# The seam between two stacks: pools ordered by lifetime, the last blocks' sum and norm as small steps of the following stack, and projections drawn ahead

## The chip, the cores and the metric

The kernel runs on one core of a Trainium2 chip, in float32 throughout. A core has a matrix engine (TensorE, PE in the profile), a vector engine (VectorE, DVE), a scalar engine (ScalarE, ACT), a general engine (GpSimd, POOL) and a queue processor (SyncE, SP) that issues most transfers. Each engine works through its own list of instructions in order; semaphores make one wait for another. The metric is the device time of one execution in microseconds (us); less is better.

## The reference

A block of two stacks over x of shape (B, S, D) = (2, 2048, 256), with a modulation that is drawn from a condition vector:

```python
mod = (silu(c) @ wmod).reshape(B, 6, 1, D)       # sa, ca, ga, sb, cb, gb
h = layernorm(x) * (1 + ca) + sa
x = x + ga * favor_stack(h)      # 3 layers: causal linear attention, 16 heads; MLP 256-1024-256
h = layernorm(x) * (1 + cb) + sb
x = x + gb * local_stack(h)      # 2 layers: attention in windows of 128, 8 heads; gated MLP
```

In the first stack each layer is post-norm: `h = LN(out + attention)`, `out = LN(h + mlp(h))`. In the second, queries, keys and values come from a token-shifted h (half the features from the token before), q and k are normalised and rotated, a softmax runs over the own and the former window, and the gated MLP follows on another token shift and norm. The third and fourth lines of the code meet at the seam of this study: the sum `x + ga * ...`, its layer norm, and the first projections of the local stack.

## The kernel before

**Two stages, two scopes.** The first `with ExitStack() as c1` holds the favor stack, the second (`c2`) the local stack. The first works in blocks of TA = 256 tokens: `favor_block(b, n)` for b in 2 batches and n in 8 blocks, three calls of `favor_layer` in each. The blocks are generators, and `planned` (L91) interleaves up to four of them by due times; the order on PE is the order in which they are drawn, while DVE, ACT and POOL of this stage are ordered by a scheduler. The local stack works in tiles of 128 tokens: `attn_tile` (L815) returns a dictionary of small operations, each with a due time in tiles in `WHEN` (L124), and all operations of all tiles, with those of the MLP (`mlp`, from L1182), are sorted by due time and drawn in that order on PE, DVE, ACT and POOL. "k" at 0.398 and "v" at 1.887, for instance, mean that a tile's k projection is drawn 0.4 tiles, and its v projection 1.9 tiles, after its q projection.

**The end of a favor block.** After layer 2, `favor_layer` returns the normed deviation `dn` (the function `normed`, L409: bn_stats and bn_aggr on DVE, Ln and Exp of the variance on ACT, subtract and multiply on DVE, L421). `favor_block` then makes `x1 = scaled(...)` (L437: three POOL operations, L442, L444 and L445, with rows that are broadcast over the partitions in `brow`), stores x1 to `xmid` in DRAM (L753), norms it again (`normed(x1)`), transposes it on PE (`turned`, L426), applies the second modulation on ACT into `hm` (L435), and stores hm to `hmid` in DRAM (L758).

**The start of the local stack.** `entry` (L789 to L795) holds the streams of 2 x 4 blocks of 512 tokens, each a tile of two rows of 512 features-by-token and a column between them for the token shift; each is loaded from `hmid` by two transfers (L794), and its shift column is copied on POOL from the block before (L783). Then come a mask (L799) and `w2` of the MLP (L199). A tile's start is: `q`, `k`, `v` (L860, two program instructions each, four in the profile), `cosq`/`cosk` (DVE, L872), `cq`/`ck`/`cv` (copies on ACT, L883 and L888), `sq` (ACT), `rot` (POOL, L902), `red` (DVE, L912), `ln` (ACT), `add` (POOL, L924), `nrm` (DVE, L929), `tp` (transposes on PE, L939), `qT` and `kT`, the scores `s0`/`s1` (L956), their maxima (L972), `ng` (L988), the exponentials (L996), `nm` (POOL, L1011), the transposes `p0`/`p1` (L1023), `av` (L1049), `oT` (DVE, L1060) and `po` (L1068).

**Memory.** The SBUF pools of the second scope take the addresses that the first scope has left, in the order in which they are opened: first the streams (`strm`, 16 tiles of 4.1 KB a partition), then weights, then work tiles. PSUM is one pool of eight banks in the second scope (`bank`, L775), taken in turn. The tag `wb1` of the shared pool holds favor layer 1's weights and later the MLP's `w1` (`load_mlp`, L184), which is loaded by `next_weights` (L721) while the favor stack still runs its last layers.

Of the kernel before, what the change touches and what calls it, by code (L numbers as in the profile page):

```python
# [14 lines left out]
P = 128  # L15
# [24 lines left out]
def block_kernel(ctx: ExitStack, tc: tile.TileContext, t: dict, out: bass.AP):  # L40
# [50 lines left out]
    def planned(jobs, at_once):  # L91
# [41 lines left out]
    }  # L133
    FEED = 0.32

    def parked(name, shape):
# [59 lines left out]

    def load_w2(pool, l):
        w2 = pool.tile([P, NFH, D], F32, tag="w2", name="w2")
        nc.sync.dma_start(  # L199
            w2[:, : NFH - 1, :], t["w2"][l, :AW, :].rearrange("(k p) n -> p k n", p=P)  # L200
        )

        for m in range(KT):
            nc.sync.dma_start(
                w2[G_AT * m : G_AT * m + GW, NFH - 1, m * P : (m + 1) * P],
                t["w2"][l, AW:, m * P : (m + 1) * P],
            )
        return w2

    attn_w, mlp_w = {}, {}  # L210


    with ExitStack() as c1:
# [9 lines left out]
        def load_x(b, n):  # L223
            xin = work.tile([P, NCA, D], F32, tag="xin", name="xin", bufs=3)
            nc.sync.dma_start(
                xin, x_in[b, n * TA : (n + 1) * TA, :].rearrange("(c p) d -> p c d", p=P)
            )
            return xin
# [177 lines left out]
            load_weights(2, "Wq", "Wk", "Wv", "Wo", "W1", "W2")  # L406
            yield 0.2, 0.0

        def normed(src):  # L409

            mv = sp.tile([P, NCA, 2], F32, tag="mv", name="mv")
            for c in range(NCA):
                bs = sp.tile([P, 6], F32, tag="bs", name="bs")
                nc.vector.bn_stats(bs, src[:, c, :])
                nc.vector.bn_aggr(mv[:, c, :], bs)
            rs = sp.tile([P, NCA], F32, tag="rs", name="rs")
            nc.scalar.activation(rs, mv[:, :, 1], AF.Ln, bias=eps_t)
            nc.scalar.activation(rs, rs, AF.Exp, scale=-0.5)
            dn = work.tile([P, NCA, D], F32, tag="dn", name="dn", bufs=3)
            for c in range(NCA):  # L420
                nc.vector.tensor_scalar(  # L421
                    dn[:, c, :], src[:, c, :], mv[:, c, 0:1], rs[:, c : c + 1], ALU.subtract, ALU.mult
                )
            return dn
# [37 lines left out]
        def favor_layer(b, n, l, h, hres):  # L462
# [245 lines left out]
            s = work.tile([P, NCA, D], F32, tag="s", name="s2")  # L708
            for c in range(NCA):
                nc.vector.tensor_tensor(s[:, c, :], acc[:, c, :], hres[:, c, :], ALU.add)  # L710
            dn = normed(s)
            yield 0.86, 3.9
            if l == LA - 1:
                return dn, None
# [17 lines left out]
        def favor_block(b, n):  # L732
            if (b, n) == (0, 0):
                dn, h = h_first
            else:
                dn = normed(early.pop((b, n)) if (b, n) in early else load_x(b, n))
                yield 0.0, 4.0
                h = hp.tile([P, KT, TA], F32, tag="h", name="h0")
                turned(dn, h, lambda k: mod[:, 1, k, b : b + 1], lambda k: mod[:, 0, k, b : b + 1])
            hres = partial(scaled, dn, R_G0 + b, R_B0 + b)  # L740
            if n > 0:
                hres = hres()
            yield 0.5, 0.9, "attention", (b, n - 1, 0) if n else None
# [21 lines left out]


    with ExitStack() as c2:

        strm = c2.enter_context(tc.tile_pool(name="strm", bufs=2 * B * NB))
        wp = c2.enter_context(tc.tile_pool(name="wF", bufs=1))  # L770
        work = c2.enter_context(tc.tile_pool(name="workF", bufs=8))
        ap_ = c2.enter_context(tc.tile_pool(name="attF", bufs=2))
        psum = c2.enter_context(tc.tile_pool(name="psF", bufs=1, space=PSUM))

        def bank(name):  # L775
            return psum.tile([P, TB], F32, tag="ps", name=name, bufs=8)

        def new_stream(b, n, before):
            s = strm.tile([P, 2 * TB + 2], F32, tag="s", name=f"s_{b}_{n}")
# [10 lines left out]
        for b in range(B):  # L790
            for n in range(NB):
                s = new_stream(b, n, entry.get((b, n - 1)))
                for kt in range(KT):
                    nc.sync.dma_start(rows(s)[kt], hmid[b, n][:, kt, :])  # L794
                entry[b, n] = s  # L795

        win_r = wp.tile([P, 2 * P], F32, name="win_r")
        for i in range(2):
            nc.gpsimd.tensor_copy(win_r[:, i * P : (i + 1) * P], win[:, (1 - i) * P : (2 - i) * P])  # L799
        w2s = {0: load_w2(wp, 0)}  # L800
        streams = [entry, {}]
        mids = [{}, {}]
        vals = {}
# [11 lines left out]
        def attn_tile(l, b, n, c):  # L815
# [68 lines left out]

            @op("cv")
            def _():
                vt = new("v", [P, INNER], bufs=5)
                nc.scalar.copy(vt, got["pq", 2])  # L888
                vals[l, b, ti] = vt

# [17 lines left out]

            @op("red")
            def _():  # L910
                ss = new("ss", [P, 2 * NH])
# [340 lines left out]
                return done and (b, n, *done)  # L1252

        steps, start = [], 0.0
        NT, NM = B * nt, B * NB * NFH
        for l in range(LF):
            for i in range(NT):
                ops = attn_tile(l, i // nt, i % nt // NCH, i % NCH)  # L1260
                steps += [(start + i + WHEN[k], l, i, f) for k, f in ops.items()]
# [135 lines left out]
```

## Time and profile before

| | us |
|---|---|
| median of the runs (2979.21 to 2981.54) | 2979.69 |
| the profiled execution | 2982.33 |
| its span, first to last instruction | 2980.5 |
| PE busy | 2909.9 (98%) |
| DVE, ACT, POOL busy | 1681.2, 1339.6, 1067.1 |
| mean granted TensorE clock | 0.99 |

The page's busy time is a mean over the span; DVE at 56% overall is at some 77% in local attention. The slices of the page cut the span into 40 parts of 74.5 us: the favor stack fills slices 0 to 20, the local stack's attention of layer 0 the slices 22 to 26, its MLP 27 to 30, and the second layer the rest.

Around the seam the chain of work that ended last runs through these steps (start, length, what):

```
1564.28 0.76 DVE s L710 x2
1566.51 0.75 DVE dn L421 x2
1567.33 1.26 POOL res L444
1568.67 1.27 POOL res L445
1571.53 0.42 DVE dn L421
1572.09 1.15 PE ntp L431 x4
1574.31 2.43 DMA h<-hm
1576.88 2.68 DMA s<-h
1579.70 6.10 PE pqkv L860 x8
```

In the timeline a row is one group of equal instructions in a row: start, the time it took, engine, line, operation, tiles, partitions x columns, how many. A float32 matmul of the program stands there as two, a transpose as one.

### The profile page before, as it was taken

The numbers are of one execution on the slowest core, as the hardware profiler recorded it, in microseconds if no ns is written. First come the engines' busy times: TensorE is split into PE (matmuls) and PEld (weight loads), VectorE is DVE, ScalarE is ACT, GpSimd is POOL, SyncE is SP. The second block draws the span as 40 slices with busy tenths as digits, with TensorE's granted clock in tenths as the row PEclk, the third lists the DMA queues.
The fourth block names the chain that finished last, engine by engine and source line by source line (L and its number), as shares of the span: only waits on it lengthen the run. The fifth ranks groups of instructions, "written<-read, shape, count | busy, mean of one in ns | idle before, by whom it ended". The sixth has DMA issues, their size and how long they took to land.

```text
span 2980.5 us, 49140 instructions
## 1 busy us (share of the span) xinstructions
PE 2909.9 (98%) x19323; PEld 2128.4 (71%) x19323; DVE 1681.2 (56%) x4186; ACT 1339.6 (45%) x3263; POOL 1067.1 (36%) x942
## 2 busy tenths in 40 slices
PE   8999999999999999999996999999999999999999
PEld 6888887888888888888784777775444777776444
DVE  5555556555665556655534777774224777775222
ACT  3343344343443334343334667665114666766211
POOL 4222233222422223322324666663002666663000
PEclk9999999999999999999998999999999999999999
DMA  6000010000100001001012000001000000000011
GB/s 217 1 1 1 8 36 15 1 1 1 43 16 1 1 1 36 22 1 43 23 34 77 1 1 1 1 1 58 0 0 10 20 1 1 2 1 8 28 43 36
DMA packets 38327, 59.48 MB, mean 20 GB/s; under 512 B 3854, under 2 KB 29008, under 8 KB 37456
## 3 DMA queue, kind: packets, MB, share of 16 engines
q1 hardware_dynamic: 36288, 52.37, 5.3%
q8 instruction: 153, 2.51, 0.3%
q0 software_dynamic: 992, 2.92, 0.3%
q10 hardware_dynamic: 816, 1.05, 0.1%
q14 instruction: 78, 0.64, 0.1%
HBM read 43.72 MB, written 12.60 MB: 19 GB/s over the span
## 4 chain that ended last, share of the span: by engine, by line
PE 89%; DVE 4%; ACT 3%; POOL 2%; issue 1%; DMA 1%; ACTq 0%; POOLq 0%; DVEq 0%; SPq 0%
PE acc L698 11%; PE pf L687 10%; PE pqkv L860 10%; PE pg L1205 5%; PE pq L475 5%; PE acc L1243 5%; PE pa L1205 4%; PE av L1049 4%; PE sim L956 3%; PE ptp L1023 3%; PE po L1068 3%; PE nd L635 3%; PE sc L563 3%; PE pu L516 3%; PE po L665 3%; PE pv L491 3%
## 5 line engine op out<-in xcount | busy, mean ns | idle before, releaser
L698 PE MATMUL acc<-wb,fr 128*128 128x256 f32 x1536 | 398.5, 382 | 7.0 <-ACT fr L695 5.1
L687 PE MATMUL pf<-h,wa 128*128 128x256 f32 x1536 | 402.4, 385 | 0.6 <-DVE att L569 0.3
L695 ACT ACTIVATE fr<-pf,vec 128x256 f32<-128x256 f32 x384 | 180.6, 471 | 427.1 <-PE pf L687 426.3
L860 PE MATMUL pqkv<-wqkv,s 128*128 128x512 f32 x768 | 357.3, 601 | 6.5 <-DMA s<-h 6.5
L569 DVE TENSOR_TENSOR att<-sc,cst 128x512 f32<-128x512 f32 x384 | 238.3, 683 | 158.0 <-PE sc L563 158.0
L698 PEld LDWEIGHTS acc<-wb,fr 128*128 128x128 f32 x1536 | 288.8, 190 | 54.0 <-ACT fr L695 8.6
L444 POOL TENSOR_TENSOR res<-dn,brow 128x512 f32<-128x512 f32 x112 | 145.1, 1295 | 486.0 <-DVE dn L421 479.4
L687 PEld LDWEIGHTS pf<-h,wa 128*128 128x128 f32 x1536 | 277.3, 191 | 55.5 <-issue 19.8
L1011 POOL TENSOR_TENSOR pm<-pm,sum 128x1024 f32<-128x1024 f32 (+1 forms) x128 | 235.5, 1840 | 179.6 <-DVE sum L1006 179.6
L996 ACT ACTIVATE pm<-pm,mx 128x256 f32<-128x256 f32 (+1 forms) x512 | 249.4, 488 | 59.2 <-DVE mx L988 59.0
L860 PEld LDWEIGHTS pqkv<-wqkv,s 128*128 128x128 f32 x768 | 138.0, 193 | 133.9 <-issue 132.0
L902 POOL TENSOR_TENSOR rot<-raw,rsn_wo 128x512 f32<-128x512 f32 x128 | 160.3, 1273 | 180.8 <-ACT raw L883 180.5
L1214 DVE SCALAR_TENSOR_TENSOR ge<-pa,vec,ge 128x512 f32<-128x512 f32 x80 | 60.1, 751 | 282.9 <-PE pa L1205 231.6
L1213 ACT ACTIVATE ge<-pg,vec 128x512 f32<-128x512 f32 x96 | 65.8, 685 | 316.5 <-PE pg L1205 316.5
L487 ACT ACTIVATE xs<-xs 64x512 f32<-64x512 f32 x192 | 120.6, 628 | 152.3 <-DVE xs L486 143.0
L1205 PE MATMUL pg<-s,w 128*128 128x512 f32 (+1 forms) x384 | 182.2, 597 | 0.0
L475 PE MATMUL pq<-h,wa 128*128 128x256 f32 x768 | 176.2, 383 | 0.7 <-ACT h L435 0.7
L486 DVE TENSOR_TENSOR xs<-pq,vec 64x512 f32<-64x512 f32 x192 | 132.1, 688 | 75.3 <-PE pq L475 71.5
L1243 PE MATMUL acc<-ge,w 128*128 128x512 f32 (+1 forms) x384 | 168.8, 600 | 0.0
L475 PEld LDWEIGHTS pq<-h,wa 128*128 128x128 f32 x768 | 146.7, 192 | 22.6 <-issue 1.4
L924 POOL TENSOR_TENSOR qk<-qk,rot 128x1024 f32<-128x1024 f32 x64 | 151.3, 2363 | 0.5
L1205 PE MATMUL pa<-s,w 128*128 128x512 f32 x320 | 150.4, 592 | 0.0
(163 smaller groups left out, 5339.7 us busy)
## 6 DMA issues: line engine op xcount, KB each, us to landing
xin<-in_x_dram SPq DMA_DIRECT2D x32, 256.0 KB, 2.8
x<-res SPq DMA_DIRECT2D x16, 256.0 KB, 2.1
h<-hm SPq DMA_DIRECT2D x16, 256.0 KB, 2.4
s<-h SPq DMA_DIRECT2D x16, 256.0 KB, 4.8
xl<-x SPq DMA_DIRECT2D x8, 512.0 KB, 4.3
out_dram<-res SPq DMA_DIRECT2D x8, 512.0 KB, 3.2
w<-in_w_dram SPq DMA_DIRECT2D x6, 640.0 KB, 3.9
wa<-in_W_dram SPq DMA_DIRECT2D x3, 1024.0 KB, 8.3
```

Of the source, the lines that this page charges most:

```text
L475: nc.tensor.matmul(pq[:, g, :], W[wn, l][:, kt, g * P : (g + 1) * P], h[:, kt, :], start=(kt == 0), stop=(kt == KT - 1),)
L569: nc.vector.tensor_tensor(am, scs[i].rearrange("p g q c -> p (g q) c"), caus.unsqueeze(1).to_broadcast([P, 2 * KT, P]), ALU.mult,)
L687: nc.tensor.matmul(pf, W["W1", l][:, kt, f * P : (f + 1) * P], h1[:, kt, :], start=(kt == 0), stop=(kt == KT - 1),)
L695: nc.scalar.activation(fr[f], pf, AF.Relu, bias=v("bf1", f))
L698: nc.tensor.matmul(acc[:, c, :], fr[f - 1][:, c * P : (c + 1) * P], W["W2", l][:, f - 1, :], start=(f == 1 and c == 0), stop=(f == NF), sk ...
L860: nc.tensor.matmul(pq, s[:, kt * TB + c * P : kt * TB + (c + 1) * P], wqkv[:, kt, i * INNER : (i + 1) * INNER], start=(kt == 0), stop=(kt ...
L902: nc.gpsimd.tensor_tensor(rot[:, :, :, lo : lo + 32], got["raw"][:, :, :, hi : hi + 32], rsn[:, ti, :, lo : lo + 32].unsqueeze(2).to_broad ...
L924: nc.gpsimd.tensor_tensor(got["qk"], got["qk"], got["rot"], ALU.add)
L996: nc.scalar.activation(pm[:, hd, :], pm[:, hd, :], AF.Exp, bias=of("mx", hg)[:, hd : hd + 1], accum_out=of("sum", hg)[:, hd : hd + 1],)
L1011: nc.gpsimd.tensor_tensor(pm, pm, of("sum", hg).unsqueeze(2).to_broadcast([P, 4, kw]), ALU.mult)
L1205: nc.tensor.matmul(pt[:m, :], w1[:, kt, off : off + m], hb[:, kt * TB : (kt + 1) * TB], start=(kt == 0), stop=(kt == KT - 1),)
L1243: nc.tensor.matmul(acc[m], w2[rs_, f, m * P : (m + 1) * P], g[rs_, :], start=(f == 0), stop=(f == NFH - 1),)
```

## The change

- **Pools.** In the second scope the work tiles (`work`), a new pool for v and the sums of squares (`vp_`) and a pool for the first four streams (`strm0`) are opened first, then the other twelve streams (`strm1`), then the rest. In the first scope, the small tiles of `normed` move from the pool `sp` to `work`.
- **The last blocks.** For the last block of each batch (n = 7), `favor_block` ends after layer 2. Its `dn` is written into a tile `last`, which takes the place of favor layer 1's weights (tag `wb1`); x of these blocks and the four rows of gains and biases are loaded there ahead. The sum, its store to `xmid`, the statistics, the norm, the transposes and the modulation become eleven steps for each batch, in the list of the local stack's layer 0 at tiles 3 + 3b to 6.6 + 3b. The tokens go straight into the stream in SBUF, not through `hmid`.
- **Streams.** Only block (0, 0) is loaded ahead of the list; the seven others are drawn at tile 1.1. The shift column comes from `hmid` by a transfer of one column instead of a copy on POOL. The mask is drawn at tile 2.
- **First projections.** `FIRST` shifts the due times of some projections of tiles 0 to 3, with the operations that take their result.
- **MLP weights.** `w1` and `w2` are loaded at tile 12 of each layer; before, layer 0's came at the end of the favor stack and the start of the local one, layer 1's at tile 4.

```diff
+    FIRST = [
+        {"v": -1.1},
+        {"q": -0.58, "k": -0.45, "v": -1.59},
+        {"q": -0.97, "k": -0.3, "v": -1.56},
+        {"q": -0.96, "k": -0.18},
+    ]
+    TAKES = {"q": ("cosq", "cq"), "k": ("ck", "cosk"), "v": ("cv",)}
...
-        def normed(src):
+        def normed(src, dn=None):
...
-            dn = work.tile([P, NCA, D], F32, tag="dn", name="dn", bufs=3)
+            if dn is None:
+                dn = work.tile([P, NCA, D], F32, tag="dn", name="dn", bufs=3)
...
-            dn = normed(s)
+            ends = l == LA - 1 and n == S // TA - 1
+            dn = normed(s, last[0][:, b] if ends else None)
...
-                mlp_w[0] = load_mlp(0)
+                room = shared.tile([P, ROOM], F32, tag="wb1", name="last")
...
+                for b in range(B):
+                    nc.sync.dma_start(
+                        last[1][:, b], x_in[b, S - TA :, :].rearrange("(c p) d -> p c d", p=P)
+                    )
+                nc.gpsimd.dma_start(
+                    last[2].rearrange("p a d -> p (a d)"),
+                    rows_out[R_GE * KT :].rearrange("a c -> (a c)").partition_broadcast(P),
+                )
...
             if n == S // TA - 1:
                 next_weights()
+                return
...
-        strm = c2.enter_context(tc.tile_pool(name="strm", bufs=2 * B * NB))
+        work = c2.enter_context(tc.tile_pool(name="workF", bufs=8))
+        vp_ = c2.enter_context(tc.tile_pool(name="valF", bufs=5))
+        strms = [
+            c2.enter_context(tc.tile_pool(name=f"strm{i}", bufs=k)) for i, k in enumerate((NB, NS - NB))
+        ]
...
+        def load_stream(b, n):
+            s = entry[b, n] = stream_tile(f"s_{b}_{n}")
+            own = slice(0, TB if n < NB - 1 else TB - TA)
+            if n == 0:
+                nc.gpsimd.memset(s[:, TB : TB + 1], 0.0)
+            else:
+                nc.sync.dma_start(s[:, TB : TB + 1], hmid[b, n - 1][:, 1, TB - 1 :])
+            for kt in range(KT):
+                nc.sync.dma_start(rows(s)[kt][:, own], hmid[b, n][:, kt, own])
+
+        load_stream(0, 0)
...
+        def last_sum(b, i):
+            dn, x, rows_ = last[0][:, b], last[1][:, b], last[2]
+            if i == 0:
+                nc.gpsimd.tensor_tensor(
+                    x, x, rows_[:, B + b].unsqueeze(1).to_broadcast([P, NCA, D]), ALU.add
+                )
+            elif i == 1:
+                nc.gpsimd.tensor_tensor(
+                    dn, dn, rows_[:, b].unsqueeze(1).to_broadcast([P, NCA, D]), ALU.mult
+                )
+            else:
+                nc.gpsimd.tensor_tensor(x, x, dn, ALU.add)
+                nc.sync.dma_start(xmid[b, NB - 1][:, NCH - NCA :, :], x)
...
+            nc.vector.bn_stats(bs, last[1][:, b, c, :])
+            nc.vector.bn_aggr(last_mv[b][:, :2, c], bs)
...
+        def last_norm(b, c):
+            m = last_mv[b][:, :, c : c + 1]
+            nc.vector.tensor_scalar(
+                last[0][:, b, c, :], last[1][:, b, c, :], m[:, 0], m[:, 2], ALU.subtract, ALU.mult
+            )
...
+        def last_tokens(b, kt):
+            nc.scalar.activation(
+                rows(entry[b, NB - 1])[kt][:, TB - TA :],
+                last_tp[b][:, kt, :],
+                AF.Identity,
+                bias=mod[:, 3, kt, b : b + 1],
+                scale=mod[:, 4, kt, b : b + 1],
+            )
...
-                if l > 0 and i == NCH:
+                when = dict(WHEN)
+                for k, shift in FIRST[i].items() if l == 0 and i < len(FIRST) else ():
+                    for k2 in (k, *TAKES[k]):
+                        when[k2] += shift
+                steps += [(start + i + when[k], l, i, f) for k, f in ops.items()]
+                if i == 3 * NCH:
                     steps.append((start + i, l, i, partial(load_mlp_late, l)))
+            if l == 0:
+                for b in range(B):
+                    steps += [
+                        (start + 3 + 3 * b + w, l, b, partial(f, b, *a))
+                        for w, f, *a in (
+                            (0.0, last_sum, 0), (0.46, last_sum, 1), (0.96, last_sum, 2),
+                            (1.5, last_stats, 0), (2.05, last_stats, 1), (2.3, last_dev),
+                            (2.5, last_norm, 0), (3.05, last_norm, 1), (3.41, last_turn),
+                            (3.42, last_tokens, 0), (3.6, last_tokens, 1),
+                        )
+                    ]
+                steps.append((start + 2.0, l, 0, turn_mask))
+                blocks = [(b, n) for b in range(B) for n in range(NB)][1:]
+                steps += [(start + 1.1, l, i, partial(load_stream, *blk)) for i, blk in enumerate(blocks)]
```

More of the change, by code (lines that the diff above doesn't have):

```diff
@@ L208, in load_w2 @@
         return w2
-    attn_w, mlp_w = {}, {}
+    attn_w, mlp_w, last = {}, {}, []
     with ExitStack() as c1:
@@ L407, in rest_of_setup @@
             yield 0.2, 0.0
-        def normed(src):
-            mv = sp.tile([P, NCA, 2], F32, tag="mv", name="mv")
+        def normed(src, dn=None):
+            mv = work.tile([P, NCA, 2], F32, tag="mv", name="mv")
             for c in range(NCA):
-                bs = sp.tile([P, 6], F32, tag="bs", name="bs")
+                bs = work.tile([P, 6], F32, tag="bs", name="bs")
                 nc.vector.bn_stats(bs, src[:, c, :])
                 nc.vector.bn_aggr(mv[:, c, :], bs)
-            rs = sp.tile([P, NCA], F32, tag="rs", name="rs")
+            rs = work.tile([P, NCA], F32, tag="rs", name="rs")
             nc.scalar.activation(rs, mv[:, :, 1], AF.Ln, bias=eps_t)
             nc.scalar.activation(rs, rs, AF.Exp, scale=-0.5)
-            dn = work.tile([P, NCA, D], F32, tag="dn", name="dn", bufs=3)
+            if dn is None:
+                dn = work.tile([P, NCA, D], F32, tag="dn", name="dn", bufs=3)
             for c in range(NCA):
@@ L725, in next_weights @@
                 attn_w[0] = load_attn(0)
-                mlp_w[0] = load_mlp(0)
+                room = shared.tile([P, ROOM], F32, tag="wb1", name="last")
+                for i in range(2):
+                    last.append(
+                        room[:, i * B * NCA * D : (i + 1) * B * NCA * D].rearrange(
+                            "p (b c d) -> p b c d", b=B, c=NCA
+                        )
+                    )
+                last.append(
+                    room[:, 2 * B * NCA * D : (2 * B * NCA + 2 * B) * D].rearrange(
+                        "p (a d) -> p a d", d=D
+                    )
[8 more added lines that the diff above has]
+                )
             elif len(late) == 2 * B:
@@ L767, in block_kernel, with stream_tile @@
     with ExitStack() as c2:
-        strm = c2.enter_context(tc.tile_pool(name="strm", bufs=2 * B * NB))
+        NS = 2 * B * NB
+        work = c2.enter_context(tc.tile_pool(name="workF", bufs=8))
[3 more added lines that the diff above has]
+        ]
         wp = c2.enter_context(tc.tile_pool(name="wF", bufs=1))
-        work = c2.enter_context(tc.tile_pool(name="workF", bufs=8))
         ap_ = c2.enter_context(tc.tile_pool(name="attF", bufs=2))
         psum = c2.enter_context(tc.tile_pool(name="psF", bufs=1, space=PSUM))
+        turns = [0]
+        def stream_tile(name):
+            k = int(turns[0] % NS >= NB)
+            turns[0] += 1
+            return strms[k].tile([P, 2 * TB + 2], F32, tag="s", name=name)
         def bank(name):
@@ L778, in new_stream @@
         def new_stream(b, n, before):
-            s = strm.tile([P, 2 * TB + 2], F32, tag="s", name=f"s_{b}_{n}")
+            s = stream_tile(f"s_{b}_{n}")
             if before is None:
@@ L789, in block_kernel, with turn_mask @@
         entry = {}
[L790 to L795, printed above, removed]
+        def load_stream(b, n):
[8 more added lines that the diff above has]
+        load_stream(0, 0)
         win_r = wp.tile([P, 2 * P], F32, name="win_r")
-        for i in range(2):
-            nc.gpsimd.tensor_copy(win_r[:, i * P : (i + 1) * P], win[:, (1 - i) * P : (2 - i) * P])
-        w2s = {0: load_w2(wp, 0)}
+        def turn_mask():
+            for i in range(2):
+                nc.gpsimd.tensor_copy(win_r[:, i * P : (i + 1) * P], win[:, (1 - i) * P : (2 - i) * P])
+        w2s = {}
         streams = [entry, {}]
@@ L886, in _ @@
             def _():
-                vt = new("v", [P, INNER], bufs=5)
+                vt = vp_.tile([P, INNER], F32, tag="v", name="v")
                 nc.scalar.copy(vt, got["pq", 2])
@@ L910, in _ @@
             def _():
-                ss = new("ss", [P, 2 * NH])
+                ss = got["ss"] = vp_.tile([P, 2 * NH], F32, tag="ss", name="ss", bufs=2)
                 nc.vector.tensor_reduce(ss, got["sq"], AX.X, ALU.add)
@@ L1252, in second, with last_stats, last_dev, last_turn @@
                 return done and (b, n, *done)
+        def last_sum(b, i):
[7 more added lines that the diff above has]
+                    dn, dn, rows_[:, b].unsqueeze(1).to_broadcast([P, NCA, D]), ALU.mult
+                )
+            else:
+                nc.gpsimd.tensor_tensor(x, x, dn, ALU.add)
+                nc.sync.dma_start(xmid[b, NB - 1][:, NCH - NCA :, :], x)
+        last_mv = {}
+        def last_stats(b, c):
+            if c == 0:
+                last_mv[b] = vp_.tile([P, 3, NCA], F32, tag="lastmv", name="lastmv", bufs=2)
+            bs = vp_.tile([P, 6], F32, tag="lastbs", name="lastbs", bufs=2)
+            nc.vector.bn_stats(bs, last[1][:, b, c, :])
+            nc.vector.bn_aggr(last_mv[b][:, :2, c], bs)
+        def last_dev(b):
+            rs = last_mv[b][:, 2, :]
+            nc.scalar.activation(rs, last_mv[b][:, 1, :], AF.Ln, bias=eps_t)
+            nc.scalar.activation(rs, rs, AF.Exp, scale=-0.5)
+        def last_norm(b, c):
+            m = last_mv[b][:, :, c : c + 1]
+            nc.vector.tensor_scalar(
+                last[0][:, b, c, :], last[1][:, b, c, :], m[:, 0], m[:, 2], ALU.subtract, ALU.mult
+            )
+        last_tp = {}
+        def last_turn(b):
+            tp = last_tp[b] = bank("ntp").rearrange("p (k c) -> p k c", k=KT)
+            for kt in range(KT):
+                for c in range(NCA):
+                    nc.tensor.transpose(
+                        tp[:, kt, c * P : (c + 1) * P],
+                        last[0][:, b, c, kt * P : (kt + 1) * P],
+                        ident,
+                    )
+        def last_tokens(b, kt):
[5 more added lines that the diff above has]
+                scale=mod[:, 4, kt, b : b + 1],
+            )
         steps, start = [], 0.0
@@ L1260, in block_kernel @@
                 ops = attn_tile(l, i // nt, i % nt // NCH, i % NCH)
-                steps += [(start + i + WHEN[k], l, i, f) for k, f in ops.items()]
-                if l > 0 and i == NCH:
-                    steps.append((start + i, l, i, partial(load_mlp_late, l)))
+                when = dict(WHEN)
[4 more added lines that the diff above has]
+                if i == 3 * NCH:
+                    steps.append((start + i, l, i, partial(load_mlp_late, l)))
+            if l == 0:
[7 more added lines that the diff above has]
+                            (3.42, last_tokens, 0), (3.6, last_tokens, 1),
+                        )
+                    ]
+                steps.append((start + 2.0, l, 0, turn_mask))
+                blocks = [(b, n) for b in range(B) for n in range(NB)][1:]
+                steps += [(start + 1.1, l, i, partial(load_stream, *blk)) for i, blk in enumerate(blocks)]
             at = start + NT
```

## The prediction

> **What bounds the kernel now.** I read the page's slices first, then busy time in stretches around the one slice that stands out, then TensorE's timeline there.
>
> ```profile
> PE   8999999999999999999996999999999999999999
> PEclk9999999999999999999998999999999999999999
> ```
>
> TensorE is full but for slice 21 (1564 to 1639 us), the seam of the two stacks. In stretches (busy us of each engine, granted clock, DMA share, GB/s):
>
> ```profile
> 1555.50:1564.20 8.70, 7.96 (x38) 6.39 (x36) 1.12 (x5) 3.32 (x9) 0.00 (x0) 1.00 0.08 31
> 1564.20:1631.40 67.20, 42.04 (x210) 24.76 (x210) 31.18 (x90) 24.06 (x69) 28.66 (x31) 0.80 0.24 85
> 1631.40:1645.40 14.00, 14.00 (x107) 10.33 (x106) 10.69 (x33) 9.43 (x28) 9.42 (x8) 1.00 0.01 2
> ```
>
> After the seam TensorE never rests: a tile of local attention is 14.0 us of 14.0. In the seam, 67.2 us hold 42.0 busy at clock 0.80. TensorE's timeline shows where (in brackets the idle time and what ended it):
>
> ```profile
> 1563.21 1.03 PE L698 MATMUL acc<-wb,fr 128*128 128x256 f32 x4
> 1572.09 1.13 PE L431 MATMUL ntp<-cst,dn 128*128 128x128 f32 x4 [7.85 <-DVE dn L421]
> 1579.70 7.80 PE L860 MATMUL pqkv<-wqkv,s 128*128 128x512 f32 x12 [6.47 <-DMA s<-h]
> 1593.47 1.97 PE L939 MATMUL tp<-cst,qk 128*128 128x128 f32 x8 [5.97 <-DVE qk L929]
> ...
> 1606.26 1.09 PE L939 MATMUL tp<-cst,qk 128*128 128x128 f32 x8 [2.93 <-DVE qk L929]
> ...
> 1619.68 2.05 PE L1068 MATMUL po<-oT,rsn_wo 128*128 128x128 f32 x16 [0.40 <-DVE oT L1060]
> ```
>
> With two waits for POOL (0.75, 0.78) the idle time is 25.2 us. The work of the stretch at full rate, from later rows: 40 projection matmuls x 0.43 (four take 1.72) = 17.2; 52 transposes x 0.109 = 5.7; sim 1.09 + 2 x 1.93 = 4.95; av 1.0 + 1.9; po 1.8; mean and var 0.55; in all 33.1. **Lost: 67.2 - 33.1 = 34.1 us**, 25.2 idle and 8.9 at half clock (twelve projection matmuls take 7.80 for 5.2).
>
> **Edit 1: sum and norm of the last blocks leave the path.** Today the chain behind the last acc is: the block's second norm (to 1567.26), POOL res 1.27 + 1.28, the norm of x1, transposes, hm (1574.3), its store 2.43, the stream load 2.68; only at 1579.70 a projection. In the changed program's order the first projection follows the last acc. It waits for wqkv and the stream of block (0,0), both early, and for the two s additions that free acc's bank, 1564.28 to 1565.04: it starts 0.85 us after acc ends. The stream's load waits for the last attention alone (nd, 1514.22 + 1.95) because its address lies where that attention's tiles were: some 45 us of cover for a load of 4.8 us (the median of s<-h). Without the cover it costs its 2.7 us landing. Also gone: 0.74 us at 1556.63, where a Relu stood on ScalarE behind x1's Ln and Exp.
>
> **Edit 2: projections ahead.** q and k of tile 0, q1, v0, k1, q2 stand first: 24 matmuls x 0.43 = 10.3, work until 11.15 (zero is acc's end). Beside it runs tile 0's chain by today's rows: DVE ends the last norm at 3.0, as now, cosq 0.70, ACT cq 0.59; k is there at 4.5, cosk 0.70, ck 0.59, so 5.8; POOL rot 2.48 and add 2.35, so 10.8; nrm 1.22, so 12.1. Idle 0.95. Transposes and v1 last to 14.7; sim waits for qT behind three ACT copies, 14.9; then q3, k2 to 19.4. Tile 1's nrm comes after POOL (rot from 13.4, add to 18.4) and eight maxima on DVE: 20.2, idle 0.8. ptp waits 0.55. av ends at 27.1, but oT stands on DVE behind the reduction and eight maxima of 0.34 (26.3 to 29.1) and ends at 29.8: idle 2.75, the largest left. What is late next is pm on POOL (0.6, 0.9, then 0.4, 0.2, 0.4 until the tiles lock in near 45). **Idle after: 0.9 + 0.95 + 0.1 + 0.8 + 0.55 + 2.75 + 2.5 = 8.6 us**, where 0.1 is the wait for qT.
>
> **Edit 3: the steps in tiles 3 to 10.** Per batch: POOL 3 x 1.27, DVE 2 x (0.41 + 0.17 + 0.41), ACT 0.5 + 2 x 0.56, TensorE 0.44, the last moved and not added. A steady tile leaves POOL 4.6 us, DVE 3.3, ACT 4.6, so these lie in gaps; the last POOL waits above are their price. Queued behind them are nm (for ptp), cosk and ng (for the exponentials); with no cover their sum would be TensorE's loss: 2 x (3.8 + 2.0 + 1.6) = 14.8 us. One of them is of a kind that blocks. dn's row, and POOL's where it was slowest:
>
> ```profile
> L421 DVE TENSOR_SCALAR dn<-s,mv,rs x192: 384/409/2295, 49.7 to 1566.8; 128x256 f32<-128x256 f32 x192
> 1480.50 6.72 POOL L172 TENSOR_TENSOR rsn_wo<-rsn_wo,rc_qks 128x1024 f32<-128x1024 f32 x2 [4.72 <-DMA rc_qks<-in_k_scale_dram]
> 1485.14 2.61 DVE L421 TENSOR_SCALAR dn<-s,mv,rs 128x256 f32<-128x256 f32 x2
> ```
>
> dn takes 0.41, but started at 1485.14 under a running POOL operation it took 2.3 and ended just after that did (1487.2). [...] By the row, a POOL that is busy 9.4 of 14.0 us with pieces of some 1.9 us makes a mean wait of 0.67 x 0.95 = 0.6 each, 2.5 in all, most of it inside DVE's 3.3 us a tile. I take **0.6** on the path, between 0 and 9.4.
>
> **Clock.** Three gaps of the old seam were followed by half clock. After it, the largest gap is 2.75. [...]
>
> ```profile
> 2029.14 1.09 PE L1023 MATMUL ptp<-cst,pm 128*128 128x128 f32 x8 [0.84 <-POOL pm L1011]
> 2031.41 1.72 PE L1023 MATMUL ptp<-cst,pm 128*128 128x128 f32 x8 [0.95 <-POOL pm L1011]
> ```
>
> Two gaps under 1 us within 3 us, and the second eight transposes take 1.72 for 1.04. So one fall of 3.4 us at half rate, 1.7 us, is likely in the seam but not sure: **1.2**, between 0 and 3.4.
>
> **Queues and rest, at nothing.** SP, in order, gets two loads of x into last (2.8 us each), six one-column loads and w2 of layer 0 between the stores of the last blocks; two hm stores go, two x stores move. No trace row has a 4-byte column; the nearest, w of 42 rows, lands in 1.9 us. They stand 40 us ahead for batch 0, and batch 1's streams, behind w2, are first read at tile 16, 220 us later; uncovered, one slot costs about 0.45 in the queue. POOL passes one more descriptor job (0.56; it lands in 7.0, over 100 us before last_sum) and six copies of 0.19 fewer. w1, w2 of layer 0 come at tile 12, 20 tiles before use; layer 1's at 12 instead of 4, the same. Uncovered they cost 3.9 once. The pools' moves of v and ss keep their buffer counts: nothing.
>
> **Sum.** 34.1 + 0.74 - 8.6 - 1.2 - 0.6 = **24.4 us less**. Of the profiled execution's own 2982.33 (span 2980.5) that leaves 2957.9; the median of the runs shown, 2979.69, lies 2.6 lower, so **2955.3**.
>
> **Rivals.**
> - *The load isn't free of the seam* (it doesn't do what it says): its address, a place in SP's order or a bank holds the first projection until after acc. Then the load, 2.7, or w2 before it, 3.9, stands open and the clock falls once (1.7): 24.4 - 4.4 to 6 = 19, 2961. For it: 6.47 <-DMA s<-h today. Against: the order puts it behind work of 1516.
> - *The steps stall the tiles*: 14.8 less the 3 counted, or 12 us: 2967. For it: TensorE has no idle time there to give, and oT is already late by 2.75. Against: POOL waits 23.3 us for DVE's sums in 1840 to 1960, 2.6 each, so its steps fill waits.
> - *Slower*: ng (L988), a tensor_scalar from SBUF too, stands between the maxima and the exponentials of each of 128 half tiles. Its row is 153/158/1126: three of 128 met POOL. If the new order shifts POOL against DVE and the shift stays, each hit costs up to 0.97 on the loop of a tile. From 26 hits (24.4 / 0.97) the gain is gone; one in each of 64 tiles is 62, so 3017. Against: from tile 4 on, the order on each engine is as before, and both seams run into a TensorE that is never idle.
>
> **Chances.** The sum 0.80 (alone 2951 to 2960), load 0.07, stall 0.07, slower 0.04, no change 0.02 by some mix. The range: 34.1 + 0.74 less 5 of idle time at best gives 2950; with the norms' 9.4 and a second fall, 2966. A measurement here tells 0.2% (6 us) from no change: faster 0.94, same 0.02, slower 0.04.
>
> **What would show it.** Right: the first projection within 1 us of the last acc, nine to ten us of them unbroken, the seam's idle time near 8.6 with oT's gap the largest, clock near 0.97 there, a 14.0 us tile from tile 4, last's POOL steps with no wait of TensorE over 1 us. Wrong: a projection that waits for DMA s<-h, last_norm over 1.5 us with av or ptp waiting, ng's median above 158, or half clock through the seam.

## The result, and the profile after

The changed kernel takes 2960.37 us (median of five runs, 2958.29 to 2961.18), the kernel before 2979.69: a ratio of 0.9934, with a 95% interval of 0.9920 to 0.9947. That is 19.3 us less, where 24.4 was forecast. The time lies within the range; the gain is a fifth smaller than the sum. The profiled execution took 2958.75 us, its span is 2957.0.

The slices of the page after, TensorE's busy tenths and its clock:

```profile
PE   8999999999999999999998999999999999999999
PEclk9999999999999999999999999999999999999999
```

Slice 21 (1552 to 1626 us here) has 8 tenths and a clock of 9, where it had 6 tenths and a clock of 8. The loss has become shorter, but it is not gone. TensorE's timeline after, at the seam (start, time, line, tiles, count; in brackets the idle time before the row and what ended it):

```profile
1558.44 1.92 PE L707 MATMUL acc<-wb,fr 128*128 128x256 f32 x8
1561.36 10.54 PE L914 MATMUL pqkv<-wqkv,s 128*128 128x512 f32 x24 [1.00 <-PE acc L707]
1572.70 1.09 PE L993 MATMUL tp<-cst,qk 128*128 128x128 f32 x8 [0.80 <-DVE qk L983]
...
1581.91 1.09 PE L993 MATMUL tp<-cst,qk 128*128 128x128 f32 x8 [1.68 <-DVE qk L983]
...
1593.74 3.78 PE L1122 MATMUL po<-oT,rsn_wo 128*128 128x128 f32 x16 [4.73 <-DVE oT L1114]
1597.31 2.30 PE L914 MATMUL pqkv<-wqkv,s 128*128 128x512 f32 x4
...
1608.79 2.05 PE L1122 MATMUL po<-oT,rsn_wo 128*128 128x128 f32 x16 [0.37 <-DVE oT L1114]
...
1612.49 1.09 PE L1077 MATMUL ptp<-cst,pm 128*128 128x128 f32 x8 [0.78 <-POOL pm L1065]
```

The three long waits (7.85, 6.47, 5.97) are gone, and 24 projection matmuls stand without a break where they were. What is left is mostly one gap of 4.73 us before tile 0's po, and behind it sixteen matmuls that take 3.78 for 1.95.

So that runs can be compared past differences that lie ahead of the seam, I cut each trace at three rows of TensorE: the end of the last acc, the start of the fourth po, and that of the eleventh. All times are us:

| kernel | last acc to 4th po | 4th to 11th po | 11th po to end | in all |
|---|---|---|---|---|
| before | 98.6 | 98.2 | 1219.5 | 1416.3 |
| after | 78.0 | 101.7 | 1217.0 | 1396.6 |

From the last acc on, the change brings 19.6 us: 20.6 in the seam, 3.5 lost in the tiles behind it, 2.5 gained later. The spans differ by 23.5, since the last acc ends 3.9 us earlier in the profile after; most of that is no gain, as the medians show: two executions of the code before, up to that row, ended it at 1564.24 and 1562.34, and executions of the changed code between 1560.21 and 1561.99.

Why is oT late? DVE's timeline after, and POOL's beside it:

```profile
1577.57 1.41 DVE L967 TENSOR_SCALAR ss<-ss 128x16 f32<-128x16 f32 x1
...
1587.91 2.36 DVE L967 TENSOR_SCALAR ss<-ss 128x16 f32<-128x16 f32 x1
...
1593.01 0.68 DVE L1114 COPY oT<-av 128x512 f32<-128x512 f32 x1
```

```profile
1576.59 2.35 POOL L978 TENSOR_TENSOR qk<-qk,rot 128x1024 f32<-128x1024 f32 x1
...
1587.89 2.35 POOL L978 TENSOR_TENSOR qk<-qk,rot 128x1024 f32<-128x1024 f32 x1
```

The clamp of the sums of squares, `ss` (L967; L913 before), works on 16 columns and usually takes 0.18 us. Twice it ended just as POOL's add ended (1578.98 beside 1578.94, 1590.27 beside 1590.24), after 1.41 and 2.36. Behind the first stands tile 1's norm, behind the second the eight maxima and oT. The same happened to `ng` (L1042; L988 before) three times in the tiles with POOL's new steps, for 0.89, 1.30 and 1.29 us. The two longest:

```profile
1636.36 1.30 DVE L1042 TENSOR_SCALAR mx<-mx 128x4 f32<-128x4 f32 x1
...
1651.85 1.29 DVE L1042 TENSOR_SCALAR mx<-mx 128x4 f32<-128x4 f32 x1
```

```profile
1636.37 1.28 POOL L1312 TENSOR_TENSOR last<-last 128x512 f32<-128x512 f32 x1
...
1651.83 1.28 POOL L1320 TENSOR_TENSOR last<-last 128x512 f32<-128x512 f32 x1
```

And it did not happen to the instruction for which the prediction had set a price. The rows of the three kinds after (count, shortest/median/longest in ns), and then the clamp's before:

```profile
L967 DVE TENSOR_SCALAR ss<-ss x64: 174/183/2357, 1568.8 to 2685.3; 128x16 f32<-128x16 f32 x64
L1042 DVE TENSOR_SCALAR mx<-mx x128: 137/157/1304, 1580.6 to 2705.0; 128x4 f32<-128x4 f32 x128
L1339 DVE TENSOR_SCALAR last<-last,lastmv x4: 399/512/621, 1628.7 to 1683.2; 128x256 f32<-128x256 f32 x4
```

```profile
L913 DVE TENSOR_SCALAR ss<-ss x64: 174/180/303, 1589.5 to 2708.2; 128x16 f32<-128x16 f32 x64
```

The medians stay; the longest tells. The clamp's 0.303 us became 2.357, in two of 64 instructions. Of ng, 5 of 128 took over 0.35 us, where it was 3 of 128 before.

### The profile page after: what moved, and what is told of

It reads as the page before. It is cut to its first block, busy times and chain, and to the rows that moved or that the text cites. A ratio compares the mean times of both kernels' runs of the same rounds, so it can differ in the third digit from the quotient of the medians.

```text
span 2957.0 us, 49152 instructions
## 1 busy us (share of the span) xinstructions
PE 2904.0 (98%) x19323; PEld 2125.8 (72%) x19323; DVE 1688.3 (57%) x4186; ACT 1339.7 (45%) x3263; POOL 1068.9 (36%) x937
## 3 DMA queue, kind: packets, MB, share of 16 engines
q0 software_dynamic: 1136, 3.44, 0.3%
q10 hardware_dynamic: 816, 1.05, 0.1%
## 4 chain that ended last, share of the span: by engine, by line
PE 88%; DVE 5%; ACT 3%; POOL 2%; issue 1%; DMA 0%; SPq 0%; DVEq 0%; ACTq 0%; POOLq 0%
PE pf L696 11%; PE acc L707 11%; PE pqkv L914 9%; PE pg L1259 6%; PE pq L484 5%; PE acc L1297 5%; PE pa L1259 5%; PE av L1103 3%; PE ptp L1077 3%; PE sim L1010 3%; PE po L1122 3%; PE nd L644 3%; PE sc L572 3%; PE pu L525 3%; PE pv L500 3%; PE po L674 3%
## 5 line engine op out<-in xcount | busy, mean ns | idle before, releaser
L1122 PEld LDWEIGHTS po<-oT,rsn_wo 128*128 128x128 f32 x1024 | 125.5, 194 | 38.1 <-issue 26.8
```

The source lines that it names most:

```text
L1122: nc.tensor.matmul(po[:, m, :], wo[:, k, m * P : (m + 1) * P], got["oT"][:, k, :], start=(k == 0), stop=(k == INNER // P - 1),)
```

## The experiments

All gains and losses below are against the changed kernel's 2960.4, unless another is named. The ratios are those to the kernel before, which ran beside each (medians 2978.6 to 2980.3). The expectations call an instruction "off the port" when it is no longer one of DVE's tensor_scalars that read and write SBUF. That is a name only: no run shows a port.

### The clamp in PSUM

In tiles 0 to 2 of layer 0 (the diff is cut to what holds in these tiles):

```diff
 @op("red")
-    ss = got["ss"] = vp_.tile([P, 2 * NH], F32, tag="ss", name="ss", bufs=2)
+    room = got["room"] = bank("rn")
+    ss = got["ss"] = room[:, 2 * NH : 4 * NH]
 @op("ln")
-    rn = got["rn"] = bank("rn")[:, : 2 * NH]
+    rn = got["rn"] = got["room"][:, : 2 * NH]
```

> In tiles 0 to 2 of layer 0 the clamp of the sums of squares (ss, L967 in the changed kernel) keeps its place and its instruction, but reads and writes a bank of PSUM instead of SBUF. Theory (blocked clamp): what the changed kernel misses in the seam is DVE's clamp, a tensor_scalar from SBUF that took 1.41 and 2.36 us for 0.2 because POOL's add qk (L978) ran until the same moment. With PSUM it takes 0.2 to 0.3 in all three tiles, the transposes of tile 1 start some 1.0 us earlier, the gap before po falls from 4.73 to under 2.8, and the clock no longer falls there: 2.3 to 4.4 us less than the changed kernel, 2956 to 2958. Rival (queue): oT is late because eight maxima and a reduction stand ahead of it, and the clamp's length is only where their wait shows; then the sum stays, within 1 us of 2960.4. Rival (clock): the gap shrinks, the half clock stays: 1.5 to 2.5 us less.

2956.24 us, ratio 0.9921 (0.9909 to 0.9934): 4.1 less. DVE and TensorE in its timeline:

```profile
1586.98 0.18 DVE L971 TENSOR_SCALAR rn<-rn 128x16 f32<-128x16 f32 x1
...
1589.86 0.70 DVE L1046 TENSOR_SCALAR mx<-mx 128x4 f32<-128x4 f32 x1
```

```profile
1580.98 1.09 PE L997 MATMUL tp<-cst,qk 128*128 128x128 f32 x8 [0.46 <-DVE qk L987]
...
1591.21 3.46 PE L1126 MATMUL po<-oT,rsn_wo 128*128 128x128 f32 x16 [3.13 <-DVE oT L1118]
```

The add that runs on POOL meanwhile:

```profile
1586.96 2.36 POOL L982 TENSOR_TENSOR qk<-qk,rot 128x1024 f32<-128x1024 f32 x1
```

The same instruction, with its operands elsewhere, takes 0.18 under the same POOL add. Tile 1's wait falls from 1.68 to 0.46, oT's from 4.73 to 3.13. Two parts of the expectation failed: the gap isn't under 2.8, because ng was now caught in the clamp's place (0.70), and the half clock stayed (3.46).

### oT ahead of the maxima

The due time of tile 0's oT, 2.958 for every other tile:

```diff
+                if l == 0 and i == 0:
+                    when["oT"] = 2.74
```

> In tile 0 of layer 0 the copy oT (L1114) is drawn right behind av and the reduction of tile 2, ahead of the eight maxima of tile 1 that it stood behind; nothing else moves. The clamp stays blocked. Theory (blocked clamp, with a queue behind it): oT starts where the clamp ends, 1590.3 for 1593.0, so the gap before po is 2.0 for 4.73; the clock then stays up or not (1.9): 2 to 4.6 us less, of which up to 0.7 comes back, as the maxima end later: 2956 to 2959. Rival (the maxima are as urgent as oT): the exponentials and pm end later by what oT gained, ptp waits in its place: within 0.7 us of the changed kernel.

2960.77 us, ratio 0.9936 (0.9924 to 0.9949): no gain; the rival held. TensorE:

```profile
1591.52 3.38 PE L1122 MATMUL po<-oT,rsn_wo 128*128 128x128 f32 x16 [1.90 <-DVE oT L1114]
...
1598.76 1.09 PE L1077 MATMUL ptp<-cst,pm 128*128 128x128 f32 x8 [0.96 <-POOL s L826]
...
1601.19 1.09 PE L1077 MATMUL ptp<-cst,pm 128*128 128x128 f32 x8 [1.11 <-POOL pm L1065]
...
1609.45 2.05 PE L1122 MATMUL po<-oT,rsn_wo 128*128 128x128 f32 x16 [1.21 <-DVE oT L1114]
```

po starts 2.8 us earlier after the last acc (30.6 for 33.4), and three waits of 0.96, 1.11 and 1.21 give it back: by the fourth po both kernels are at 78.0. So the queue's order was not the fault, its length was.

### POOL's additions left out, and ng on ScalarE

The first leaves out the three operations of `last_sum` in each batch, so it computes something else. The second keeps all and moves ng of tiles 0 to 9 to ScalarE (cut in the same way):

```diff
 @op("ng0", "ng1")
-    nc.vector.tensor_scalar(of("mx", hg), of("mx", hg), -1.0, None, ALU.mult)
+    nc.scalar.mul(of("mx", hg), of("mx", hg), -1.0)
```

> The six POOL operations of the last blocks' sum (L1312, L1316, L1320) are left out; statistics, norm, transposes and tokens stay, from x alone. Theory (steps block ng): in the changed kernel ng (L1042), another tensor_scalar from SBUF, took 0.89, 1.30 and 1.29 us for 0.16 while such an addition ran, and ptp waited 0.78, 0.99 and 0.64 us for pm behind it; without them 1.5 to 3 us less than the changed kernel, 2957.5 to 2959. Rival (steps lie in gaps, as the prediction had it for all but the norms): within 0.6 us. Rival (last_norm is what blocks): it stays, within 0.6 us, and last_norm takes over 1 us; in the changed kernel it took 0.40 to 0.62.

> The changed kernel with ng of tiles 0 to 9 on ScalarE; the clamp stays in SBUF. Theory (the steps' price is ng caught by their POOL additions, and nothing else): from the start of po of the fourth tile to that of the eleventh it takes 99.3 us, as with both off the port, for 101.7; the gaps of 1.68 and 4.73 in the seam stay; 2 to 3.5 us less than the changed kernel, 2957 to 2958.5. Rival (the clamp's place in tiles 3 to 9 made that difference): that stretch stays at 101.7, within 1 us of the changed kernel.

Without the additions: 2959.25 us, ratio 0.9931 (0.9917 to 0.9944), 1.1 less, between theory and rival. With ng on ScalarE: 2958.18 us, ratio 0.9923 (0.9910 to 0.9937), 2.2 less. The cuts say what the totals hide: from the 4th to the 11th po the two take 99.7 and 99.3 for 101.7, as the theory had it, but the seam takes 79.8 and 79.0 for 78.0. In both, a clamp that had been free in the changed kernel was now caught: tile 3's, 1.96 and 1.97 us. To take one collision away shifts POOL against DVE and can make another. last_norm took 0.40 to 0.63 in both; it isn't the cause.

### Projections ahead undone

```diff
-    FIRST = [
-        {"v": -1.1},
...
+    FIRST = []
```

> The projections ahead are undone (FIRST is empty); pools and steps stay. Theory (they cover tile 0's chain through DVE, ACT and POOL): the waits before the transposes of tiles 0 and 1 go back from 0.80 and 1.68 to near the old 5.97 and 2.93, and the clock falls once more: 6.4 to 9 us more than the changed kernel, 2967 to 2969. Rival (the same projections only come later, and the work they would have covered is covered by others): under 3 us more.

2965.01 us, ratio 0.9950 (0.9938 to 0.9963): 4.6 more, less than expected. The old waits are back:

```profile
1572.54 1.97 PE L988 MATMUL tp<-cst,qk 128*128 128x128 f32 x8 [5.91 <-DVE qk L978]
...
1584.44 1.09 PE L988 MATMUL tp<-cst,qk 128*128 128x128 f32 x8 [2.94 <-DVE qk L978]
```

But no clamp is caught in this order, and po waits 1.21 for oT, not 4.73. (Of ng, three are caught up to the fourth po, for 0.82 to 1.28, where the changed kernel has one of 0.89.) To draw projections ahead brings the waits of 5.91 and 2.94 down to 0.80 and 1.68, and pays for it with the clamps; 4.6 us is what remains.

### Edit 1 undone, and the pools undone

In the first, the norm of the last blocks stands in the favor stack again (no `return` behind `next_weights()`, no `last`, no eleven steps, whole streams loaded from `hmid`). In the second, `strm` is one pool of 16 tiles again, opened ahead of `work`.

> Edit 1 is undone: the last blocks' sum, norm, transposes and store stand in the favor stack again, before the first projection in TensorE's order; pools, streams at tile 1.1 and projections ahead stay. In the program's order the load of stream (0,0) still waits only for the last attention, not for the last store. Theory (two waits of the old seam have two owners): the wait for dn comes back (7.85 for 1.00), with 0.74 at a Relu, 0.44 of transposes and one fall of the clock (1.7), but not the 6.47 for the stream's load, which the pools and the split loads took away: 7 to 10 us more than the changed kernel, 2967.5 to 2970.5. Rival (the load belongs to the last blocks too): both waits come back, 15 us or more, over 2975.

> The streams are one pool of sixteen again, opened first, so their addresses lie where the favor stack's last work was; steps and projections ahead stay. In the program's order the load of stream (0,0) then waits for the last pf matmul of the favor stack, which ended at 1558.6, 1.8 us before the last acc. Theory (pools free the load): the load lands 3.0 to 4.5 us after that, so the first projection starts 2.2 to 3.7 us after the last acc and not 1.0: 1.2 to 2.7 us more than the changed kernel, and 1.7 more where that gap makes the clock fall: 2961.5 to 2965. Rival (pools do nothing): within 0.6 us of the changed kernel.

Edit 1 undone: 2970.86 us, ratio 0.9970 (0.9959 to 0.9982), 10.5 more, just above the theory's end.

```profile
1570.20 1.13 PE L440 MATMUL ntp<-cst,dn 128*128 128x128 f32 x4 [7.85 <-DVE dn L430]
1572.49 12.49 PE L892 MATMUL pqkv<-wqkv,s 128*128 128x512 f32 x24 [1.16 <-ACT hm L444]
```

The wait for dn is back to the hundredth, that for the stream is not: as the theory said, it had another owner, and the projections start 1.16 after the transposes, though at half clock at first (12.49 for 10.54). Without the steps the 4th to 11th po take 98.2, as before.

Pools undone: 2961.76 us, ratio 0.9940 (0.9928 to 0.9953), 1.4 more, a number inside the expectation for a reason outside it:

```profile
1562.73 10.54 PE L910 MATMUL pqkv<-wqkv,s 128*128 128x512 f32 x24 [1.04 <-DMA s<-h]
```

The first projection now waits for the load, and still starts 1.04 us after acc, for 1.00: the load landed just in time. (In the kernels with the new pools this start lies at 1.00 to 1.05.) The loss is elsewhere, a caught clamp in tile 3:

```profile
1606.53 1.96 DVE L963 TENSOR_SCALAR ss<-ss 128x16 f32<-128x16 f32 x1
```

The pools' order gives the load room; in this kernel that room was not needed.

### The clamp in PSUM with ng on ScalarE, and the gap filled

The clamp in PSUM and ng on ScalarE, in tiles 0 to 9; then, added to it, k of tile 3 ahead of po of tile 0:

```diff
-        {"q": -0.96, "k": -0.18},
+        {"q": -0.96, "k": -0.3},
```

> In tiles 0 to 9 of layer 0 the clamp reads and writes PSUM, and ng (mx) is made by ScalarE instead of DVE; POOL's steps stay. Theory (what the steps cost is ng caught by them): beside the 4.1 us of the clamp alone, the three or four long ng (0.70, 0.88, 1.29, 1.28 in that run) are gone, and with them the waits of ptp for pm of 0.8, 1.0 and 0.6: 1.5 to 3 us less than with the clamp alone, 2953 to 2955. Rival (POOL's own time is what makes pm late): the waits for pm stay, within 0.6 us of the clamp alone. Rival (ScalarE pays): ng there takes 0.2 us and delays the exponentials: no gain, or a loss to 1 us.

> The kernel with both caught instructions off the port, and k of tile 3 drawn before po of tile 0 instead of behind it. Theory (the gap before po is too long for the clock): the four projection matmuls, 1.88 us, fill most of the 2.6 to 3.1 us gap, no window is idle enough, po takes 1.95 for 3.46: 1.5 to 3.5 us less than without the move. Rival (pm of tile 1 is the next limit and takes the gap): ptp waits for pm instead, under 0.7 us.

Both moved: **2951.22 us, ratio 0.9903 (0.9888 to 0.9918), 9.1 us less than the changed kernel**, more than the 5.6 to 7.1 expected. From the last acc: 72.7 us to the 4th po, 99.3 from there to the 11th, 1216.9 to the end. In these two traces that is 7.8 us less from the last acc on; the medians stand over executions that differ by some 3 us among themselves. No clamp and no last_norm in this stretch is over 0.63 us. With the gap filled, 2951.81 us, ratio 0.9908 (0.9894 to 0.9921): the same, as the rival said. TensorE there:

```profile
1588.55 1.98 PE L914 MATMUL pqkv<-wqkv,s 128*128 128x512 f32 x4
1591.20 2.02 PE L1129 MATMUL po<-oT,rsn_wo 128*128 128x128 f32 x16 [0.67 <-ACT pm L1057]
...
1594.40 1.09 PE L1084 MATMUL ptp<-cst,pm 128*128 128x128 f32 x8 [0.31 <-POOL s L826]
...
1596.83 1.09 PE L1084 MATMUL ptp<-cst,pm 128*128 128x128 f32 x8 [1.11 <-POOL pm L1072]
```

po takes 2.02 with a gap of 0.67, for 3.39 with one of 2.53, so the theory's clock was right; but ptp, which waits for tile 1's pm, takes most of it back. The same stretch after, and in this kernel (span; busy PE, PEld, DVE, ACT, POOL; granted clock, DMA share, GB/s):

```profile
1562.00:1605.00 43.00, 35.54 (x186) 22.05 (x186) 29.68 (x75) 22.31 (x65) 27.14 (x24) 0.92 0.19 59
```

```profile
1562.00:1605.00 43.00, 39.14 (x224) 24.03 (x225) 31.39 (x92) 25.79 (x80) 30.25 (x25) 1.00 0.19 60
```

### The same edit on the kernel before, and a shorter queue

> The kernel before, with the clamp of tiles 0 to 9 in PSUM and ng of these tiles on ScalarE; nothing of the change. Theory (what was caught was caught because the change puts POOL's add and its steps beside these instructions): before, the clamps of the seam took 0.23 to 0.27 us and one ng 0.82, so there is next to nothing to win: within 1.5 us of the kernel before, where the same edit took 9.1 us off the changed kernel. Rival (the edit is worth its 9 us to any order, by less work on DVE): 5 us less or more.

2975.62 us, ratio 0.9984 (0.9976 to 0.9993): 4.3 us less than before, so neither expectation held. The cuts give 97.0, 98.2 and 1216.9 for 98.6, 98.2 and 1219.5. Some 1.6 lies in the seam, where the one ng of 0.82 is gone. Of the later 2.6, 1.6 lies in one tile whose waits did not change and which only the clock makes shorter (see the last section). The remaining 1.0 lies behind the last tile that the edit touches. So 2.6 of the 4.3 is no work of the edit that I can name. The changed kernel does not have that fall of the clock; so of the 9.1 us that the edit brought it, at most 2.7 may have been there for the taking before.

The last two try to shorten DVE's queue ahead of po: tile 2's reduction behind tile 1's maxima and oT (0.905 and 0.96 stand for 0.655 and 0.760), without and with the filled gap.

```diff
+                if l == 0 and i == 0:
+                    when["oT"] = 2.86
+                if l == 0 and i == 2:
+                    when["red"], when["ln"] = 0.905, 0.96
```

> The kernel with both caught instructions off the port, and on DVE the reduction of tile 2 (red, with its clamp, and ln on ScalarE) is drawn behind the eight maxima of tile 1 instead of ahead of them, and oT of tile 0 between them. TensorE's order is the same. Theory (the rest of the gap before po is DVE's queue: 1.2 of reduction, 0.2 of clamp, 2.8 of maxima): maxima, pm and oT all come 1.0 us earlier, the gap before po falls from 2.53 to about 1.5, and the clock perhaps stays up (1.4): 1 to 2.4 us less than without the move, 2949 to 2950. Rival (the norm of tile 2, now later, is the next limit): tp or the next ptp waits in its place: within 0.7 us.

> The last kernel, with k of tile 3 drawn before po of tile 0 as well. Theory (with pm 1 us earlier, ptp no longer takes back what the filled gap gave): clock 1.00 through the seam, waits of ptp for pm under 0.8 in all, and 1 to 2 us less than with either move alone: 2948 to 2949.5. Rival (pm stays the limit): as with the reduction moved alone, within 0.7 us.

2953.70 us, ratio 0.9912 (0.9898 to 0.9925), and 2954.25 us, ratio 0.9914 (0.9900 to 0.9927): 2.5 and 3.0 more than with both moved. po starts 0.8 us earlier (28.8 for 29.6 after the last acc). In the first, a wait of 1.08 for pm in a later ptp takes it back; in the second the clock stays up, but tp waits 1.07 for tile 2's norm and two ptp 1.81 and 1.11. By the 4th po both are 0.8 us later. The rest of the loss, some 1.9 us in the traces, lies behind the 11th po, far from the edit.

## Why the prediction was right, and what was wrong in its sum

**Edit 1.** Right. The first projection starts 1.00 us after the last acc (0.85 predicted), the Relu's 0.74 us is gone, and no store or load of the last blocks stands on the path; with edit 1 undone 10.5 us come back.

**The load's cover.** Right in the outcome, wrong in the price: "without the cover it costs its 2.7 us landing". Measured: 0.04, which is no more than the kernels with the new pools differ among themselves.

**Edit 2, the idle times.** 9.8 us came for 8.6. Tile 0's transposes waited 0.80 (0.95), ptp 0.25 (0.55), what came late from there to the 4th po cost 1.3 (2.5). Two terms were too small: tile 1's transposes, 1.68 for 0.8, and oT, 4.73 for 2.75. The step that failed is "oT stands on DVE behind the reduction and eight maxima": the clamp that stands between them has no price there beyond the 0.18 of its row before. It cost 2.36, and the one of the tile before it 1.41. With the clamp in PSUM the two waits are 0.46 and 3.13.

**Edit 3.** 0.6 predicted; the 4th to 11th po take 3.5 us more. Of these 0.87 are the last blocks' transposes, which moved there; 2.6 are a real loss, and with ng off DVE 2.4 of them go (99.3). Clamp and ng waited here until a POOL operation ended, and took up to 2.36 and 1.30 us for 0.18 and 0.16; why they wait no trace shows. I set the price of such a wait on the wrong instruction. I asked which *added* tensor_scalar from SBUF would meet POOL, and named last_norm, which took 0.40 to 0.62. The 9.4 us at the upper end of the range, four norms at 2.36 each, no run shows: in the profile after the four took 2.04 together. The added POOL operations met the tensor_scalars that were *already there*. The rival "slower" named ng and the price of a hit (up to 0.97; 0.73 to 1.14 were measured), with 26 hits as the point from which it decides. In all, five came for three before, and two of the clamp.

**Clock.** 1.2 predicted, 2.2 measured (3.78 and 2.30 for 1.95 and 1.88). The row of before (two gaps under 1 us, then 1.72 for 1.04) pointed the right way: the clock fell behind gaps of 4.73 (changed kernel), 3.13 (clamp in PSUM), 2.53 (both moved), 1.90 (oT ahead) and 1.75 us (shorter queue). But the length of a gap does not decide by itself: behind 1.68 (changed kernel) and 1.81 (gap filled, shorter queue) it did not fall. In all 14 traces, the granted clock changes only at multiples of 3.41 us from one another. From 1500 us to the last 8 us there are 22 falls; in the step of 3.41 us just before each, TensorE was busy for 1.66 us or less. Of the steps at full clock without a fall behind them, one had 1.61 and all others 1.69 or more. In the profiles before and after alone there are five falls, with 1.63 or less in the step ahead, and no other step at full clock has less than 1.69. The fall at 2031.7 in the profile before, with the step ahead of it and the one behind it:

```profile
2028.30:2031.70 3.40, 1.61 (x14) 1.42 (x14) 1.77 (x4) 3.37 (x7) 3.06 (x3) 1.00 0.00 0
2031.70:2035.10 3.40, 3.40 (x17) 2.24 (x15) 0.69 (x1) 0.02 (x1) 0.00 (x0) 0.50 0.02 5
2035.10:2038.50 3.40, 3.40 (x10) 1.42 (x8) 0.00 (x0) 1.40 (x3) 0.33 (x1) 1.00 0.00 0
```

So it matters how a gap lies against these steps, and that differs between executions: the last acc ends 74.8 us (21.9 steps) behind the fall at 1485.5 in the profile after, and 76.6 us (22.4 steps) behind that at 1485.0 with the pools undone, though TensorE's work up to there is the same. The clock term of a single trace is one draw.

**"8.9 at half clock".** Not all of that was clock. In the kernel with the filled gap, at clock 1.00, the stretch to the 4th po takes 71.4 us with 5.1 idle: 66.3 of work. The sum had 33.1 + 31.45 (1631.40 to the fourth po) - 0.44 (transposes moved out) = 64.1. These 2.2 us are rows that stand at a wait or a change of operands: eight transposes then take 1.09 and eight projection matmuls 3.70, where in the unbroken pace the next row starts 0.87 and 3.44 us after them (1636.59 to 1637.46 and 1645.39 to 1648.83 in the profile before). Row by row this comes to 2.1. The seam of before had about as much. Beside the rows of 7.80 and 1.97 (shown with the prediction), these two of it ran at half clock:

```profile
1595.24 3.37 PE L860 MATMUL pqkv<-wqkv,s 128*128 128x512 f32 x4
...
1608.72 3.46 PE L860 MATMUL pqkv<-wqkv,s 128*128 128x512 f32 x4
```

At full clock the four take 5.38, 1.09, 1.88 and 1.88, so the clock makes 6.4 of the 8.9. What restarts cost was there before and is there after, and I had counted it as gain.

**Behind the seam**, 2.5 us were won that the sum did not have, 1.6 of them one fall of the clock that the execution before shows and the one after does not. For the other 0.9 no cause was found. This is luck, and it hid more than a third of what the sum had too high.

Together: 1.2 (idle) + 1.0 (clock) + 2.2 (restarts) + 2.0 (steps) + 0.4 (transposes from ahead of the last acc) - 2.5 (later) = 4.3 us less than forecast from the last acc on; measured 23.7 - 19.6 = 4.1. Of the rivals, "the load isn't free" and "no change" fell, and "the steps stall the tiles" holds for 2.6 of its 12 us.

## What to carry to other kernels

When work moves to POOL or POOL moves in time, list every tensor_scalar on DVE that reads and writes SBUF in the stretch, however small: its price here was not its own length (0.18 and 0.16 us) but up to that of the POOL operation it met (2.36 beside 2.35, 1.30 beside 1.28), and everything behind it in DVE's queue. A small operand can be kept in PSUM or the instruction put on another engine; here that was worth 9.1 us by the medians and 7.8 in the traces, beside 19.3 for the whole change. And when lost time is split into idle time and slow clock, take a stretch at full clock with the same waits first: what restarts cost, 2.2 us here, is in neither.

## What was not expected of the hardware

An instruction of 16 columns waited 2.2 us, and one of 4 columns 1.1, each for a POOL operation that started within 0.02 us of it. The four others in the profile after that waited met one that had started 0.41 to 1.28 us earlier. All seven ended within 0.04 us of it.

The same instructions with the same waits can meet half clock or not. In the profile before, the waits of 0.84 and 0.95 at 2029 and 2031 (shown with the prediction) are followed by transposes that take 1.72. After, in the same tile:

```profile
2008.16 1.09 PE L1077 MATMUL ptp<-cst,pm 128*128 128x128 f32 x8 [0.84 <-POOL pm L1065]
...
2010.43 1.09 PE L1077 MATMUL ptp<-cst,pm 128*128 128x128 f32 x8 [0.95 <-POOL pm L1065]
```

The six tiles around it take 96.8 us in the profile before, 96.9 in that with edit 1 undone, and 95.2 or 95.3 in all the others, whose code in this stretch is the same. In the two kernels with the shorter queue it is layer 1's tile that is caught; the first of them:

```profile
2686.39 1.09 PE L1084 MATMUL ptp<-cst,pm 128*128 128x128 f32 x8 [0.84 <-POOL pm L1072]
2688.65 1.79 PE L1084 MATMUL ptp<-cst,pm 128*128 128x128 f32 x8 [0.95 <-POOL pm L1072]
```

So a kernel can gain or lose 1.6 us by how its waits lie against the clock's steps (see "Clock" above), far from what was edited. Whether that comes out the same in every execution of a kernel was not measured; the control's runs (2973.88 to 2977.32), which lie below all those of the kernel before beside them (2977.84 to 2982.63), point to it, but they hold other gains as well.
